# One set of accumulator pools for the whole kernel: keeping three PSUM pairs across the seam into the MLP

## The chip, the cores and the metric

The kernel runs on one core of a Trainium2 chip. The metric is the time of one execution on the device in microseconds (us). The engines are named as in the profile: PE is TensorE (PEld its weight loads), DVE is VectorE, ACT is ScalarE, POOL is GpSimd and SP is SyncE[...]. PE writes its results into a memory of its own, PSUM[...]. In this kernel nearly every PSUM tile is a pair of banks (128 x 2 x 512).

## The reference

Two layers act on `x` of shape (2, 512, 32, 32), all in float32. Cut to what matters:

```python
# layer 0: deformable attention with a bias from a small network, then an MLP
xn = bn(x); q = gconv1x1(xn, qw)
off = tanh(conv1x1(gelu(conv_dw(q)))) * 4
kv = grid_sample(xn, grid(off)); k, v = gconv1x1(kv, kw), gconv1x1(kv, vw)
bias = relu(relu(slog(pos) @ w1 + b1) @ w2 + b2) @ w3 + b3   # 16 groups x 1024 x 64 positions, width 128
attn = softmax(scale * q @ k.T + bias)
x = x + conv1x1(attn @ v, out_w) + out_b
x = x + mlp_w2 @ gelu(mlp_w1 @ bn(x) + mlp_b1) + mlp_b2      # 512 -> 2048 -> 512, 2 x 1024 positions
# layer 1: plain attention over 1024 positions, width 512
q, k, v = x @ Wq.T + bq, x @ Wk.T + bk, x @ Wv.T + bv
x = x + softmax(q @ k.T / sqrt(512)) @ v @ Wp.T + bp
```

## The kernel before

The kernel has four stretches, and a scheduler orders the instructions of each engine; it places all waits on semaphores itself, from what each tile's users are.

*The main loop* (lines 778 to 841) computes the bias network: 256 steps, each of four tiles `ps` (L635) of 128 x 2 x 512 in PSUM, evicted by ACT (L644, L646) and summed by DVE and by adding transfers. The logits are gathered in tiles `sim` of one bank each. Two PSUM pools exist for it, opened at L132: `simp` with two single banks for the logits, and `zp` with three pairs for everything else. In the built program `simp` lies in banks 0 and 1, `zp` in banks 2 to 7.

*The output projection* (`project`, L894) and all later matrix products are done with seven products of half-sized blocks in place of eight (`PARTS`, L98). `multiply` (L116) runs through the products in a given order: it takes a tile from a pool, calls `product`, which issues the matmuls, and then hands the tile to a function that evicts it, mostly a DVE addition (`plus`, L122) or an ACT copy. A product of the projection or the MLP is eight PE instructions. `project(0)` and `project(1)` (L1030, L1037), one for each image of the batch, take their tiles from `zp`, in the order 1, 2, 5, 6, 7, 3, 4.

*The MLP* (loop at L1044) has eight units, four for each image. A unit has `layer1` (L959; order 1, 6, 7, 4, 5, 3, 2, with evictions into `hm` and a gelu on ACT, L962) and `layer2` (L992; order 3, 2, 1, 5, 6, 7, 4). Its tiles come from a third pool, `mq`, of four pairs. It is opened at L1042, after the loop at L1040 has closed `zp` and `simp`, and covers their eight banks. In the built program its first tile is in banks 0 and 1, and the next three are in 6, 4 and 2.

For each unit the loop also prepares a part of layer 1's biases: L1051 transfers 256 KB of a weight into `wr`, and DVE multiplies it by a row and sums it (L1060). `wr` has one buffer, so each transfer waits for the L1060 before it. The scheduler puts all eight of these L1060 early: five of them stand among the evictions of `project(0)` and `project(1)`, and three among those of the first unit's layer 1. The weights of a unit (`w1t`, `w2t`, 1 MB each) are loaded by `load_unit` (L877) and completed by POOL (L105), as is `gg` (L846), 1 MB, which the attention of layer 1 needs later.

*The attention of layer 1* (from L1073) takes its tiles from `mq` as well.

Of the kernel before, what the change touches and what calls it, by code (L numbers as in the profile page):

```python
# [12 lines left out]
PSUM = bass.MemoryType.PSUM  # L13
# [26 lines left out]
for _name, _w in _VCOLS:  # L40
    VOFF[_name] = _n
    _n += _w
NV = _n


@with_exitstack
def conv_seq_kernel(ctx: ExitStack, tc: tile.TileContext, x, xt, kst, pst, cst, vec, wsm, outw, w1, w2, wl, wlt, brow, out):
# [7 lines left out]
    ident = cp.tile([P, P], F32, name="ident")  # L55
    vs = cp.tile([P, NV], F32, name="vs")
    nc.scalar.dma_start(out=vs, in_=vec)
# [71 lines left out]
        x = [q[:, k : k + 2, n : n + 512] for k in (0, 2) for n in (0, 512)]  # L129
        return w + [wsum[:, j] for j in range(3)], x + [parts[:, j] for j in range(3)]  # L130

    simpp, zpp = (tc.tile_pool(name=n, bufs=c, space=PSUM) for n, c in (("simp", 2), ("zp", 3)))  # L132
    simp, zp = simpp.__enter__(), zpp.__enter__()

    def flat(name):
        return zp.tile([P, 2, 512], F32, tag="ps2", name=name).rearrange("p h n -> p (h n)")
# [4 lines left out]
    with tc.tile_pool(name="lp", bufs=2) as lp:  # L141
# [389 lines left out]
        def weights(i):  # L531
            ps = [flat("psg") for _ in range(2)]
            for o in range(NCH):
                for k in range(NCH):
                    if i == 0 and (o, k) in ((1, 0), (3, 1)):
                        yield
                    nc.tensor.matmul(  # L537
                        ps[k // 2][:, k % 2 * 512 : k % 2 * 512 + 512], wls[i][:, 0, o, k * P : (k + 1) * P],
                        wls[i][:, 1, o, :], start=(o == 0), stop=(o == NCH - 1),
                    )  # L540
            yield
            for k2 in range(2):
                nc.scalar.copy(gs[:, i, 2 * k2 : 2 * k2 + 2, :].rearrange("p k o -> p (k o)"), ps[k2])
            yield
            nc.gpsimd.dma_start(out=gdr[i], in_=gs[:, i])
# [4 lines left out]
        head, g, n = chain(0), weights(0), weights(1)  # L550
# [321 lines left out]
    with ExitStack() as top, tc.tile_pool(name="wp", bufs=2) as wp:  # L872
# [4 lines left out]
        def load_unit(b, p):  # L877
            ws_ = []
            for i, w in enumerate((w1, w2)):
                wt = wp.tile([P, 7, 2, 256], F32, name=f"w{i + 1}t")  # L880
                nc.sync.dma_start(out=wt[:, 0:4], in_=w[:, p])
                fold(nc.gpsimd, [wt[:, j] for j in range(7)])
                ws_.append(wt)
            wts[b, p] = ws_

        for i, (b, h) in enumerate(halves):
            for o in range(NCH):
                n = slice(h * 512, (h + 1) * 512)
# [148 lines left out]
        project(1, *op1, op1w[:, 3:5].rearrange("p a k n -> p a (k n)"))  # L1037
        spread([xb[:, j] for j in range(7)])
        load_unit(*units[1])
        for pl in (zpp, simpp):  # L1040
            pl.__exit__(None, None, None)
        mqp = tc.tile_pool(name="mq", bufs=4, space=PSUM)  # L1042
        mq = mqp.__enter__()
        for i, (b, p) in enumerate(units):  # L1044

            j, k = divmod(i, NCH)
# [28 lines left out]
    with tc.tile_pool(name="sp", bufs=1) as sp:  # L1075
# [3 lines left out]
        for b in range(B):  # L1079
# [171 lines left out]
            multiply(mq, (1, 2, 6, 7, 5, 3, 4), product(vt, at, nk=4), {  # L1251
                1: a1, 2: a2, 6: a6, 7: a7, 5: a5, 3: a3, 4: a4,
            })
    mqp.__exit__(None, None, None)


def _constants(np):
# [112 lines left out]
```

## Time and profile before

Three timed runs gave a median of 2648.25 us (2647.37 to 2648.81).

| | |
|---|---|
| time of the profiled execution | 2648.76 us |
| its span on the core | 2647.0 us |
| PE busy | 2628.8 us (99%) |
| DVE busy | 2240.1 us (85%) |
| ACT busy | 1693.2 us (64%) |
| POOL busy | 791.0 us (30%) |
| main loop, about | 0 to 1890 us |
| projection | about 1890 to 1949 us |
| MLP | 1952 to 2339 us |
| attention of layer 1 | 2339 to 2642 us |

A busy share is an average over these four stretches. What one seam costs is read from the engines' timelines around it: when an engine's last instruction ended, when its next one started, and what released it. In the rows of a timeline, a bracket at the end gives the idle time before the row and the instruction or transfer that ended it. Lines of helpers stand for many callers: L123 is every DVE eviction by `plus`, so rows are told apart by the tile they write (`xs` and `op1w` in the projection, `hm` in layer 1 of the MLP).

### The profile page before, as it was taken

What the parts mean: (1) busy time and instruction counts of PE and PEld (TensorE: products, weight loads), DVE (VectorE), ACT (ScalarE), POOL (GpSimd) and SP (SyncE); (2) the same over time, 40 slices, a digit from 0 to 9 for tenths busy, and PEclk for the clock granted to TensorE, in tenths of its full rate; (3) what the DMA queues carried; (4) which work ended last, traced back from release to release, by engine and by line L of the source; (5) the groups of instructions that cost most, each with busy time, mean ns of one, the idle gap of its engine ahead of it and who ended that gap; (6) DMA issues with size and microseconds to landing.
All of it is one profiled execution on the core that took longest, in us unless ns stands there. A gap on an engine that the chain in (4) does not pass through costs nothing.

```text
span 2647.0 us, 46958 instructions
## 1 busy us (share of the span) xinstructions
PE 2628.8 (99%) x19368; PEld 953.9 (36%) x19368; DVE 2240.1 (85%) x1329; ACT 1693.2 (64%) x2222; POOL 791.0 (30%) x867
## 2 busy tenths in 40 slices
PE   9999999999999999999999999999999999999999
PEld 3333322333333233233333323333334444446454
DVE  7999999999999999999999999999674483466354
ACT  5887898888888878887887777777521131114041
POOL 1333333333333333333333333333432232000000
PEclk9999999999999999999999999999999999999999
DMA  5788977888878888887887888788721111000000
GB/s 188 178 178 173 199 166 167 179 182 197 177 169 180 178 178 193 173 177 169 182 183 169 176 177 182 168 174 185 193 96 33 47 48 48 0 17 0 32 1 32
DMA packets 116294, 366.77 MB, mean 139 GB/s; under 512 B 23376, under 2 KB 27616, under 8 KB 113392
## 3 DMA queue, kind: packets, MB, share of 16 engines
q0 software_dynamic: 69408, 235.31, 47.3%
q1 hardware_dynamic: 46240, 128.15, 13.7%
q8 instruction: 153, 2.51, 0.4%
q14 instruction: 61, 0.50, 0.1%
q10 hardware_dynamic: 432, 0.31, 0.0%
HBM read 74.81 MB, written 6.55 MB: 31 GB/s over the span
## 4 chain that ended last, share of the span: by engine, by line
PE 92%; DVE 3%; issue 2%; ACT 2%; DMA 1%; DVEq 0%; POOL 0%; SPq 0%; ACTq 0%; POOLq 0%
PE ps L635 62%; PE sw L953 15%; PE sw L1084 9%; PE sw L1182 2%; PE sim L721 1%; PE psg L537 1%; DVE h L618 1%; PE sw L900 1%; DVE ub L654 0%; DMA wr<-in_wlt 0%; PE pkv L471 0%; DVE xs L908 0%; PE sim L704 0%; PE pt L738 0%; DMA uc<-uo 0%
## 5 line engine op out<-in xcount | busy, mean ns | idle before, releaser
L635 PE MATMUL ps<-h,cw 128*32 128x512 f32 x16384 | 1776.4, 592 | 5.2 <-ACT rx L644 4.0
L618 DVE CUSTOM_DVE_ANT_1 h<-ta,tb 128x4096 f32<-128x4096 f32 (+1 forms) x257 | 1131.2, 4402 | 28.6 <-PE ps L635 25.8
L635 PEld LDWEIGHTS ps<-h,cw 128*32 128x32 f32 x16384 | 543.0, 110 | 1203.1 <-issue 1131.4
L644 ACT ACTIVATE rx<-ps,sc 128x1024 f32<-128x1024 f32 x512 | 567.9, 1109 | 145.1 <-PE ps L635 127.1
L646 ACT ACTIVATE ub<-ps,sc 128x1024 f32<-128x1024 f32 x256 | 308.2, 1204 | 93.6 <-PE ps L635 93.5
L654 DVE SCALAR_TENSOR_TENSOR ub<-rx,sc,ub 128x1024 f32<-128x1024 f32 x256 | 327.1, 1278 | 6.6 <-ACT ub L646 6.6
L673 POOL DMA_DIRECT2D ua<-uc x126 | 158.8, 1275 | 298.6 <-DMA ua<-uc 288.7
L673 POOL DMA_DIRECT2D ua<-ua x189 | 225.9, 1372 | 16.8 <-DMA ua<-uo 11.9
L953 PE MATMUL sw<-xb,w1t 128*128 128x512 f32 x448 | 195.2, 596 | 3.1 <-DVE xs L123 3.1
L656 POOL DMA_DIRECT2D uo<-ub x127 | 125.6, 989 | 233.0 <-DVE ub L654 217.8
L953 PE MATMUL sw<-hm,w2t 128*128 128x512 f32 x448 | 193.6, 592 | 0.0
L646 ACT ACTIVATE uo<-ps,sc 128x1024 f32<-128x1024 f32 x128 | 154.2, 1204 | 53.0 <-PE ps L635 52.7
L654 DVE SCALAR_TENSOR_TENSOR uo<-rx,sc,uo 128x1024 f32<-128x1024 f32 x128 | 163.7, 1279 | 9.0 <-ACT uo L646 9.0
L123 DVE TENSOR_TENSOR hm<-hm,sw 128x1024 f32<-128x1024 f32 x56 | 67.5, 1218 | 105.5 <-PE sw L953 105.3
L673 POOL DMA_DIRECT2D uc<-uo x63 | 53.6, 852 | 313.5 <-DMA uc<-uo 307.4
L953 PEld LDWEIGHTS sw<-xb,w1t 128*128 128x128 f32 x448 | 85.7, 192 | 111.5 <-issue 105.7
L962 ACT ACTIVATE hm<-hm,vs 128x512 f32<-128x512 f32 x64 | 42.5, 713 | 129.0 <-DVE hm L123 129.0
L953 PEld LDWEIGHTS sw<-hm,w2t 128*128 128x128 f32 x448 | 85.1, 190 | 107.1 <-issue 106.4
L123 DVE TENSOR_TENSOR xs<-xs,sw 128x1024 f32<-128x1024 f32 (+1 forms) x48 | 55.6, 1171 | 73.7 <-PE sw L1084 36.0
L656 POOL DMA_DIRECT2D ua<-ub x64 | 58.6, 915 | 179.1 <-DVE ub L654 171.8
L1084 PE MATMUL sw<-aT,vt 128*128 128x512 f32 x224 | 96.7, 593 | 0.3 <-ACT aT L1164 0.3
L987 ACT COPY hm<-sw 128x1024 f32<-128x1024 f32 x8 | 8.1, 1010 | 136.3 <-PE sw L953 136.3
(247 smaller groups left out, 2268.2 us busy)
## 6 DMA issues: line engine op xcount, KB each, us to landing
uo<-ub POOLq DMA_DIRECT2D x127, 512.0 KB, 5.5
fb<-fdr SPq DMA_DIRECT2D x64, 512.0 KB, 5.1
ua<-ub POOLq DMA_DIRECT2D x64, 512.0 KB, 5.5
uc<-ub POOLq DMA_DIRECT2D x64, 512.0 KB, 5.1
ua<-ua POOLq DMA_DIRECT2D x63, 256.0 KB, 6.2
ua<-uo SPq DMA_DIRECT2D x63, 256.0 KB, 2.6
ua<-uo POOLq DMA_DIRECT2D x63, 256.0 KB, 5.7
uc<-uc POOLq DMA_DIRECT2D x63, 256.0 KB, 6.7
```

The lines of the kernel that those rows point to most:

```text
L123: nc.vector.tensor_tensor(out, a, b_, op)
L618: nc.vector._custom_dve(TENSOR_ADD_SAT, out=h1[:, y : y + step].rearrange("p y t x -> p (y t x)"), in0=a.unsqueeze(1).to_broadcast([P, ste ...
L635: nc.tensor.matmul(ps[32 * q : 32 * q + 32, h, :], cw2[:, 32 * z : 32 * z + 32], h1[:, 16 * h : 16 * h + 16, q, :], start=True, stop=True,)
L644: nc.scalar.activation(o, ps, AF.Relu, bias=sc[:, 4 + z : 5 + z])
L646: nc.scalar.activation(o, ps, AF.Relu, bias=sc[:, 4 + z : 5 + z], scale=sc[:, z : z + 1])
L654: nc.vector.scalar_tensor_tensor(r[1], r[0], sc[:, z : z + 1], r[1], ALU.mult, ALU.add)
L656: nc.gpsimd.dma_start(out=sums[s][1], in_=sums[s][3], accum_op=ALU.add)
L673: nc.gpsimd.dma_start(out=out, in_=in_, accum_op=ALU.add)
L953: nc.tensor.matmul(ps[:, m, :], w[:, a, k, m * P : (m + 1) * P], x[:, b_, k, :], start=(k == 0), stop=(k == 1),)
L962: nc.scalar.activation(hm[:, blk, m, :], src[:, m, :], AF.Gelu, bias=col("mb1", 4 * p + 2 * (blk // 2) + m), scale=scale,)
L1084: nc.tensor.matmul(ps[:, m, :], w[:, a, k, c + m * P : c + (m + 1) * P], x[b_][:, k, :], start=(k == 0), stop=(k == nk - 1),)
L1182: nc.tensor.matmul(v[:, m, :], xbl[b_][:, k, m * P : (m + 1) * P], gn[:, a, k, :], start=(k == 0), stop=(k == 1),)
```

## The change

`zp` is opened first and stays open to the end of the kernel; `simp` is opened after it, so that in the built program the pairs lie in banks 0 to 5 and the logits in 6 and 7. At the start of the MLP only `simp` is closed. A pool of one pair is opened in its place, and a small class, `Turns`, takes tiles in turn: one from the new pair, then three from `zp`, and so on. The number of pairs from the MLP on is four, as before.

```diff
+class Turns:
+    def __init__(self, pools):
+        self.pools = pools
+
+    def tile(self, *args, **kw):
+        self.pools = self.pools[1:] + self.pools[:1]
+        return self.pools[-1].tile(*args, **kw)
...
-    simpp, zpp = (tc.tile_pool(name=n, bufs=c, space=PSUM) for n, c in (("simp", 2), ("zp", 3)))
-    simp, zp = simpp.__enter__(), zpp.__enter__()
+    zp = ctx.enter_context(tc.tile_pool(name="zp", bufs=3, space=PSUM))
+    simpp = tc.tile_pool(name="simp", bufs=2, space=PSUM)
+    simp = simpp.__enter__()
...
-        for pl in (zpp, simpp):
-            pl.__exit__(None, None, None)
-        mqp = tc.tile_pool(name="mq", bufs=4, space=PSUM)
-        mq = mqp.__enter__()
+        simpp.__exit__(None, None, None)
+        mq = Turns([ctx.enter_context(tc.tile_pool(name="mq", bufs=1, space=PSUM)), zp, zp, zp])
...
-    mqp.__exit__(None, None, None)
```

## The prediction

> **What bounds the kernel now.** I read the page's busy shares and chain first, then TensorE's waits, then the seam between the projection and the MLP engine by engine. TensorE (PE) is busy 2628.8 of 2647.0 us. From the start of the MLP to the end the chain of waits is almost only matmuls, and it reaches that start by way of a transfer and VectorE (DVE). From the chain in order of time (start, length, what):
>
> ```profile
> 1946.29 4.01 DMA wr<-in_wlt
> ...
> 1951.13 1.14 DVE xs L123
> 1952.27 0.04 issue
> 1952.32 386.35 PE sw L953 x896
> 2338.67 72.10 PE sw L1084 x168
> ```
>
> The waits of PE from 1950 us on (total, times, longest) show the one stall there:
>
> ```profile
> PE sw L953 <- DVE xs L123: 3.1, 1, 3.1
> PE sw L1084 <- ACT aT L1164: 0.3, 2, 0.2
> ```
>
> The timeline of PE (start, duration, count) places it: the last product of `project(1)` (L900), then the first unit's layer 1 (56 instructions are seven products of eight), then its layer 2.
>
> ```profile
> 1945.60 3.60 PE L900 MATMUL sw<-op1x,vp 128*128 128x512 f32 x8
> 1952.32 25.85 PE L953 MATMUL sw<-xb,w1t 128*128 128x512 f32 x56 [3.12 <-DVE xs L123]
> 1978.00 7.46 PE L953 MATMUL sw<-hm,w2t 128*128 128x512 f32 x17
> ```
>
> A second loss hangs on the first. The table of stretches for L953 (length, PE busy, PEld busy, granted clock, DMA share, GB/s) shows the clock halved after the stall:
>
> ```profile
> 1949.20:1952.30 3.10, 0.00 (x0) 0.00 (x0) 0.96 0.81 276
> 1952.30:1955.70 3.40, 3.38 (x5) 1.52 (x6) 0.53 0.97 380
> 1955.70:1959.00 3.30, 3.30 (x9) 1.51 (x8) 1.00 1.04 354
> ```
>
> DVE's timeline through the same time is what decides how much of this can be won:
>
> ```profile
> 1950.43 0.69 DVE L1060 SCALAR_TENSOR_TENSOR wr<-wr,br 128x512 f32<-128x512 f32 x1 [0.77 <-DMA wr<-in_wlt]
> 1951.05 0.08 DVE L1060 DVE_READ_ACCUMULATOR wr<-wr,br 128x1 f32 x1
> 1951.05 1.22 DVE L123 TENSOR_TENSOR xs<-xs,sw 128x1024 f32<-128x1024 f32 x1
> 1961.11 1.22 DVE L123 TENSOR_TENSOR hm<-hm,sw 128x1024 f32<-128x1024 f32 x1 [8.85 <-PE sw L953]
> 1962.38 1.61 DVE L1060 SCALAR_TENSOR_TENSOR wr<-wr,br 128x512 f32<-128x512 f32 x1
> ...
> 1966.74 1.37 DVE L1060 SCALAR_TENSOR_TENSOR wr<-wr,br 128x512 f32<-128x512 f32 x1 [1.05 <-DMA wr<-in_wlt]
> ...
> 1970.87 1.39 DVE L1060 SCALAR_TENSOR_TENSOR wr<-wr,br 128x512 f32<-128x512 f32 x1 [1.61 <-DMA wr<-in_wlt]
> ```
>
> The reader is to see that L1060, a row of work that the MLP doesn't need, stands between the evictions in DVE's queue, and each time waits for a transfer into a single buffer. The transfer for the L1060 of 1962.38 was issued at 1953.12 behind 3 MB of weights (w2t, w1t, gg); the DMA view of 1953 to 1954 us gives its time to landing:
>
> ```profile
> wr<-in_wlt SPq DMA_DIRECT2D x1, 256.0 KB, 9.2
> ```
>
> So it landed at about 1962.3. It was no bound before, since the eviction ahead of it ended at 1962.33.
>
> [...] the idles of 1.67 and 0.81 us at 1927 and 1935 us cost no clock. [...]
>
> **The change part by part.** In the built program every engine has the same instructions in the same order in both kernels; waits differ at six. Before, the first MLP product waits for the last eviction of `project(1)` (DVE, 1951.05 to 1952.27), though its own banks, the logits', had long been free: the new pool waited for all of the old ones. After, product 1 waits for its weights alone. Product 6 (second in order) waits for the eviction of product 7 of the projection (ends 1945.12), product 7 for that of product 3 (1949.66), product 4 for the last (1952.27). ScalarE (ACT) drops its DVE wait before copying product 1. One L1060 gains a wait for the L1060 before it, done at 1951.13; I cost it at nothing, the hm eviction ahead of it ends later, and at most a 0.05 us queue row if not.
>
> *Gain at the seam.* Products follow each other every 3.43 us (1938.73 to 1942.16), so PE could go on at 1945.60 + 3.43 = 1949.03, and starts at 1952.32: 3.29. In the slow clock, from the first matmul to that of the second product takes 5.09 us (second product at 1952.32 + 5.09 = 1957.41 by its weight loads, 0.43 apart), against 3.51 after the short stall at 1935.22 (next product 1938.73): 1.58. Filling the pipeline again is the other 0.08. Sum 4.95. No new buffer wait follows: PE wants the buffers of products 6, 7 and 4 at 1952.46, 1955.89 and 1959.32, all later than their evictions. The inputs are older still: normalised xb is complete at 1940.7, the folded w1t at 1915.8.
>
> *What is late next.* Layer 1 would end, and layer 2 want to begin, at 1949.03 + 7 x 3.43 = 1973.04. Its first matmul reads hm[3], so it needs ACT's gelu (L962), which needs the first DVE eviction of product 5, which stands behind three L1060 in DVE's queue. The first hm eviction moves from 1961.1 to 1956.0, but the L1060 behind it still can't start before 1962.3 (landing) and takes 1.61. It frees the buffer, and the next transfer lands 2.6 us later (1966.7); L1060 takes 1.37; again a transfer (1970.9) and 1.39. This chain is tied to the transfers and not to PE, so it doesn't move: the eviction of product 5 starts at 1972.18 and the gelu at 1973.43 as before. From ACT:
>
> ```profile
> 1973.43 1.33 ACT L962 ACTIVATE hm<-hm,vs 128x512 f32<-128x512 f32 x2 [2.80 <-DVE hm L123]
> ```
>
> Two halves of 0.71 us lie in that row; PE needs the first at its start: 1973.43 + 0.71 + 0.05 of handover (as from 1952.27 to 1952.32 in the chain) = 1974.2. The second ends at 1974.76, PE reaches it at 1975.1. So PE stalls 1974.2 - 1973.04 = 1.2 us, and with the 0.08 of refilling gives back 1.25. After that the evictions of products 3 and 2 are done at about 1975.7 and 1976.9 and the gelu of hm[0] at 1978.4, before PE wants it at 1981.1; the other units have no L1060, and their loads are issued when PE frees a buffer, so they move with it.
>
> *Sum.* 4.95 - 1.25 = 3.70 us. The profiled execution took 2648.76 us (span 2647.0 and 1.76 around it): 2645.06. The three timed runs have a median of 2648.25, 0.51 lower; less 3.70 that is 2644.55. I take 2644.8, between them.
>
> **The rivals.** *A, the whole 4.95 is won:* the wr transfer lands 1.2 us or more earlier. For it: the DMA rate already falls to some 50 GB/s at 1960 us, so little is left to move then. Against: nothing in the change moves the transfer or its issue. 2648.76 - 4.95 = 2643.8, by the median 2643.3. *B, the stall only moves:* the transfer lands 2 us later, the new stall is above 3 us, and the clock drops there too: 4.95 - 3.2 - 0.08 - 1.58 = 0.1 gained, 2648.7. For it: it was issued into full queues and its delay is no fixed number. Against: the queues were empty from 1962.0 on (0 GB/s in a table of stretches), and the two later transfers take 2.6 each. *C, slower:* the pairs move from banks 2-7 to 0-5 and the logits from 0-1 to 6-7, in the whole main loop. Were an eviction or a matmul group dearer there, it counts 1024 times (512 + 256 + 128 of the page's ACT rows, and more in rows it leaves out). The gain is gone at 3.70 / 1024 = 3.6 ns a tile; at 10 ns the time is 2648.76 - 3.70 + 10.24 = 2655.3. Against: L635 on three pairs and L953 on all four, the logits' place included, both have 592 ns a matmul. Unknown from both sides, below nothing too; I take zero.
>
> **How the numbers follow.** Main case 0.63, A 0.18, B 0.13, C 0.06. About 0.2% (5.3 us) is what a measurement of this kernel can tell from no change; faster by more than that means below 2642.95, which none of the cases gives by its own sum, so it takes A and a low run, or the main case with gains I don't see: 0.12. C gives slower: 0.06. The rest, 0.82, is within. The range, 2643.0 to 2647.2, holds the main case with a landing 1.2 us earlier to 2 us later without the clock drop (2643.8 to 2647.1) and A by the median.
>
> **What would show it.** Right: the first L953-type matmul starts at about 1949.0, the clock stays at 1.00 there, the first L1060 after the first hm eviction now waits for its transfer (about 5 us), and a new PE stall of about 1.2 us before layer 2, released by ACT's gelu. Wrong: a PE start above 1950, a clock below 1 after the seam, layer 2 beginning at 1973.1 (A) or after 1975.5 (B), or another time at 1945 us (C).

## The result, and the profile after

| | before | after |
|---|---|---|
| median of 12 runs each, us | 2649.26 | 2645.77 |
| lowest to highest, us | 2646.70 to 2651.06 | 2643.40 to 2648.08 |
| time of the profiled execution, us | 2648.76 | 2645.56 |
| its span, us | 2647.0 | 2643.8 |

The ratio of the times is 0.9984, with a 95% interval of 0.9977 to 0.9992: 0.16% faster, which is within the 0.2% band, as forecast. One later execution of the changed kernel, of 21 in e10, ran at a clock of 0.556 and took 4672.46 us; the ratios are taken without it. Lines of the changed kernel are 12 higher than before (11 for the evictions: L123 became L134). The lines that answer to those shown of before follow.

The chain of waits of the changed kernel (start, length, what) now runs from the projection into the MLP with nothing between matmuls; the transfer and the DVE pieces that stood before the MLP are gone.

```profile
1939.58 11.16 PE sw L912 x26
1950.73 384.71 PE sw L965 x896
2335.44 72.10 PE sw L1096 x168
```

TensorE's waits after 1940 us (total, times, longest): the 3.1 us on the eviction is no longer there.

```profile
PE sw L1096 <- ACT aT L1176: 0.3, 2, 0.2
```

Its timeline (start, duration, operation, count) gives the two distances that matter. The MLP starts 1950.57 - 1947.14 = 3.43 us after the last product, which is one product. Layer 2 starts 1974.70 - 1950.57 = 24.13 us later, where seven products take 24.03.

```profile
1947.14 3.60 PE L912 MATMUL sw<-op1x,vp 128*128 128x512 f32 x8
1950.57 24.20 PE L965 MATMUL sw<-xb,w1t 128*128 128x512 f32 x56
1974.70 10.54 PE L965 MATMUL sw<-hm,w2t 128*128 128x512 f32 x24
```

The table of stretches for L965 (length, PE busy, weight loads, granted clock, DMA share, GB/s) has the full clock, where before had 0.53:

```profile
1950.50:1953.90 3.40, 3.33 (x8) 1.52 (x8) 1.00 0.82 274
1953.90:1957.30 3.40, 3.40 (x9) 1.52 (x8) 1.00 1.00 389
```

DVE's timeline (the bracket is the idle time before a row, and what ended it) shows the sums, now L1072, late behind their transfers, as the prediction said:

```profile
1957.71 1.22 DVE L134 TENSOR_TENSOR hm<-hm,sw 128x1024 f32<-128x1024 f32 x1 [4.17 <-PE sw L965]
1962.68 1.72 DVE L1072 SCALAR_TENSOR_TENSOR wr<-wr,br 128x512 f32<-128x512 f32 x1 [3.75 <-DMA wr<-in_wlt]
...
1967.19 1.34 DVE L1072 SCALAR_TENSOR_TENSOR wr<-wr,br 128x512 f32<-128x512 f32 x1 [1.65 <-DMA wr<-in_wlt]
...
1971.27 1.39 DVE L1072 SCALAR_TENSOR_TENSOR wr<-wr,br 128x512 f32<-128x512 f32 x1 [1.60 <-DMA wr<-in_wlt]
```

And ACT's gelu of hm[3], which layer 2 needs first:

```profile
1973.84 1.33 ACT L974 ACTIVATE hm<-hm,vs 128x512 f32<-128x512 f32 x2 [2.80 <-DVE hm L134]
```

Half of this row is done after 0.71 us, and 0.05 us of handover makes 1974.60. TensorE could begin layer 2 at 1950.57 + 24.03 = 1974.60. The two meet: the 1.25 us that the prediction takes off for this wait isn't lost here, though the chain behind it is there in full.

What lies ahead of the seam was 1.54 us later in this execution (last projection product at 1947.14 against 1945.60): the projection began 1.17 us later (1896.54 against 1895.37) and took 0.37 longer. In the main loop, which the change doesn't touch but for the place of its banks, TensorE was busy 395.45 us of the stretch 200 to 600 us against 397.03. So 3.2 us of span are gained, though the seam itself gained 4.8. Repetitions of either kernel spread over 4 us, so single spans can't settle a term of 1 us; the distances around the seam can.

### The profile page after: what moved, and what is told of

The parts are those of the page before. It is cut to its first block, busy times and chain, and to the rows that moved or that the text cites. A ratio compares the mean times of both kernels' runs of the same rounds, so it can differ in the third digit from the quotient of the medians.

```text
span 2643.8 us, 46960 instructions
## 1 busy us (share of the span) xinstructions
PE 2626.8 (99%) x19368; PEld 942.7 (36%) x19368; DVE 2240.6 (85%) x1329; ACT 1692.8 (64%) x2222; POOL 791.8 (30%) x867
## 4 chain that ended last, share of the span: by engine, by line
PE 93%; DVE 3%; ACT 2%; issue 2%; DMA 0%; DVEq 0%; ACTq 0%
PE ps L647 62%; PE sw L965 15%; PE sw L1096 9%; PE sw L1194 2%; PE sim L733 1%; PE psg L549 1%; PE sw L912 1%; DVE h L630 1%; DVE ub L666 0%; DVE xs L920 0%; PE pkv L483 0%; PE sim L716 0%; PE pt L750 0%; DVE acc L346 0%; ACT ub L658 0%
## 5 line engine op out<-in xcount | busy, mean ns | idle before, releaser
L647 PEld LDWEIGHTS ps<-h,cw 128*32 128x32 f32 x16384 | 532.4, 110 | 1215.5 <-issue 1140.4
L965 PE MATMUL sw<-hm,w2t 128*128 128x512 f32 x448 | 193.6, 592 | 0.0
L965 PE MATMUL sw<-xb,w1t 128*128 128x512 f32 x448 | 193.6, 592 | 0.0
L134 DVE TENSOR_TENSOR hm<-hm,sw 128x1024 f32<-128x1024 f32 x56 | 67.4, 1218 | 98.0 <-PE sw L965 97.6
L965 PEld LDWEIGHTS sw<-hm,w2t 128*128 128x128 f32 x448 | 85.0, 190 | 107.4 <-issue 106.4
L965 PEld LDWEIGHTS sw<-xb,w1t 128*128 128x128 f32 x448 | 85.1, 190 | 107.1 <-issue 105.2
L134 DVE TENSOR_TENSOR xs<-xs,sw 128x1024 f32<-128x1024 f32 (+1 forms) x48 | 55.6, 1170 | 72.9 <-PE sw L1096 36.0
L610 ACT ACTIVATE ta<-fb,vs 128x512 f32<-128x512 f32 (+1 forms) x65 | 89.3, 1376 | 10.8 <-DMA fb<-fdr 10.8
```

The source lines that it names most:

```text
L134: nc.vector.tensor_tensor(out, a, b_, op)
L610: nc.scalar.activation(ta.rearrange("p j x -> p x j")[:, :, j0:j1], fb[:, 0, :, j0:j1], AF.Identity, bias=col("cb1"), scale=col("w1x"),)
L647: nc.tensor.matmul(ps[32 * q : 32 * q + 32, h, :], cw2[:, 32 * z : 32 * z + 32], h1[:, 16 * h : 16 * h + 16, q, :], start=True, stop=True,)
L965: nc.tensor.matmul(ps[:, m, :], w[:, a, k, m * P : (m + 1) * P], x[:, b_, k, :], start=(k == 0), stop=(k == 1),)
```

## The experiments

They are read by two distances. The first goes from the start of the projection's last product to the start of layer 2. Without any loss it is 3.43 + 24.03 = 27.46 us; what is above that is lost at the seam or before layer 2 ("lost"). The second ("whole") goes from the start of the projection's first product to the start of layer 2, and so has the stalls of the projection in it too. The last column says where the slow clock shows: after the longest stall of the projection (at about 1928 us), where eight matmuls then took 5.40 us and not 3.70, or at the start of the MLP, where the table of stretches has 0.53. Starts in us, from TensorE's timeline of each profile:

| kernel | first product | last product | MLP | layer 2 | lost | whole | slow clock |
|---|---|---|---|---|---|---|---|
| before | 1895.37 | 1945.60 | 1952.32 | 1978.00 | 4.94 | 82.63 | MLP |
| before, a second execution (e7) | 1895.97 | 1947.03 | 1952.64 | 1978.47 | 3.98 | 82.50 | both |
| before, banks as after (e1) | 1895.72 | 1946.93 | 1952.95 | 1977.09 | 2.70 | 81.37 | projection |
| before, stall filled (e2) | 1895.61 | 1946.95 | 1953.61 | 1977.75 | 3.34 | 82.14 | none |
| before, late sums (e8) | 1896.75 | 1948.25 | 1953.16 | 1977.30 | 1.59 | 80.55 | projection |
| after | 1896.54 | 1947.14 | 1950.57 | 1974.70 | 0.10 | 78.16 | none |
| after, a second execution (e0) | 1895.62 | 1946.82 | 1950.25 | 1974.28 | 0.00 | 78.66 | none |
| after, a third (e10) | 1898.12 | 1949.58 | 1953.01 | 1977.04 | 0.00 | 78.92 | projection |
| after, more stores (e4) | 1895.07 | 1945.29 | 1948.73 | 1973.33 | 0.58 | 78.26 | none |
| after, late sums (e3) | 1895.50 | 1946.96 | 1950.39 | 1974.42 | 0.00 | 78.92 | projection |
| four pairs in the projection (e5) | 1895.13 | 1942.70 | 1946.14 | 1973.00 | 2.84 | 77.87 | none |
| four pairs, late sums (e6) | 1896.08 | 1943.32 | 1946.76 | 1970.79 | 0.01 | 74.71 | none |
| the same, a second execution (e9) | 1897.84 | 1945.07 | 1948.51 | 1972.54 | 0.01 | 74.70 | none |

The two distances are needed together, because a loss can move from the projection to the seam. TensorE's last product comes later where the projection had its slow clock, while the last eviction that DVE owes it comes no later (it ended 56.6 to 57.2 us after the projection's first product in before, e7 and e1 alike); the stall at the seam is then shorter, and nothing is won by that. In the mean of three executions of each kernel (before, e7 and e1 against after, e0 and e10) the whole fell from 82.17 to 78.58 us, by 3.59, which is what the medians show.

My theory was that of the prediction: the stall and the clock are won, and the sums in DVE's queue give 1.25 us back before layer 2. The rivals were A (nothing is given back), B (the stall moves to layer 2 and costs the clock there) and C (the new bank places cost something in each tile).

### The changed kernel again, twice (e0, e10)

> The changed kernel once more, for how far its seam varies. Theory (the gain is the seam's stall of 3.3 us and the slow clock's 1.6 us; what is given back depends on when the sixth wr transfer lands): the first MLP matmul starts 3.43 us after the last projection product, clock 1.00, and layer 2 starts 24.0 to 25.3 us after that, 24.0 where the transfer lands less than about 12.1 us after the first MLP matmul, 25.3 where it lands 13.3 us after it. Rival (the gain sits elsewhere, in the main loop or the banks): the seam varies by microseconds, or the main loop ends earlier than before's 1890 us.

> The changed kernel again beside these two, for its ratio on the same chip: 0.9977 to 0.9992 as measured first; in its profile layer 2 24.0 to 24.5 us after layer 1 starts (a stall before layer 2 of at most 0.4 us, where the prediction said 1.2).

One execution gave 2645.05 us. The third profile came with 20 more timed runs: 2645.47 us median of all 21, ratio 0.9985 (0.9978 to 0.9992), as at first. Neither lost anything before layer 2. So in the three executions of the changed kernel that were profiled, the give-back is 0.0 to 0.1 us, not 1.25.

### Only the bank places (e1)

```diff
-    simpp, zpp = (tc.tile_pool(name=n, bufs=c, space=PSUM) for n, c in (("simp", 2), ("zp", 3)))
+    zpp, simpp = (tc.tile_pool(name=n, bufs=c, space=PSUM) for n, c in (("zp", 3), ("simp", 2)))
...
-        for pl in (zpp, simpp):
+        for pl in (simpp, zpp):
```

> Before with the banks of the changed kernel alone (pairs in banks 0 to 5, logits in 6 and 7), all pools still closed and a new one opened at the seam. Theory (bank places cost nothing, the gain is the seam): the time of before, ratio 1.000 within 0.0007; PE stalls 3.1 us at the seam and the clock is near 0.5 for 3.4 us. Rival (the gain or a loss is in the banks): 0.998 as the changed kernel, or above 1.001.

2649.43 us, ratio 0.9998 (0.9990 to 1.0006). The upper end is 0.0006 x 2649 = 1.6 us, over 1024 tiles at most 1.6 ns a tile; rival C needed 3.6 to take the gain away. It is out. The experiment says nothing of the cause of the stall: every wait in the built program is as before, and the MLP's first tile is again in banks 0 and 1, which are now those of the projection's last product, so here its own banks call for the same wait.

The profile brought something else. A stall of 3.1 us with a slow clock was expected. The stall is still there, but shorter, and no slow clock follows it. TensorE's timeline, then the table of stretches for L953:

```profile
1946.93 3.60 PE L900 MATMUL sw<-op1x,vp 128*128 128x512 f32 x8
1952.95 24.30 PE L953 MATMUL sw<-xb,w1t 128*128 128x512 f32 x56 [2.42 <-DVE xs L123]
```

```profile
1952.90:1956.30 3.40, 3.35 (x8) 1.63 (x9) 1.00 0.96 400
```

### The kernel before again (e7)

> The kernel before once more, to see how constant its losses at the seam are. The profile read for the prediction had a stall of 3.1 us and then 3.4 us at a clock of 0.53; the kernel with its pairs in other banks had 2.4 us and no slow clock. If the length of the stall decides: a stall near 3.1 us comes with a slow clock, one under 2.5 us without. [...] Span 2645 to 2648 us.

2649.23 us. The stall was shorter still, 2.01 us, and the clock did drop:

```profile
1947.03 3.60 PE L900 MATMUL sw<-op1x,vp 128*128 128x512 f32 x8
1952.64 26.00 PE L953 MATMUL sw<-xb,w1t 128*128 128x512 f32 x56 [2.01 <-DVE xs L123]
```

```profile
1952.60:1956.00 3.40, 3.36 (x4) 1.41 (x5) 0.53 0.99 390
```

The same execution had a slow clock already in the projection, after a shorter stall still, and the changed kernel had none there after a longer one. Eight matmuls took 5.40 us in the first and 3.70 in the second:

```profile
1928.06 5.40 PE L900 MATMUL sw<-qa,vp 128*128 128x512 f32 x8 [1.86 <-DVE xs L123]
1928.83 3.70 PE L912 MATMUL sw<-qa,vp 128*128 128x512 f32 x8 [2.06 <-DVE xs L134]
```

So the length of the stall alone doesn't decide: 1.86 us was enough here and 2.42 was not in e1. What else does isn't shown by these runs. The loss at this seam before was 4.94, 3.98 and 2.70 us in three executions with the same order of instructions (before, e7 and e1), 3.87 in the mean. The prediction's 4.95 is the worst of the three.

The timed runs give no place for a drop, only the mean clock of the whole kernel. One drop (3.4 us at 0.53) lowers it by 3.4 x 0.47 / 2647 = 0.0006; among the 13 profiles, those with no drop have a mean clock of 1.000 (e0 alone 0.999), those with one 0.999 and the one with two 0.998. Of the 102 runs of before that stood beside the experiments, 28 have 1.000, 51 have 0.999 and 23 have 0.998, with mean times of 2648.4, 2649.6 and 2651.0 us. Of the 53 timed runs of the changed kernel with and without late sums (after, e10 but for the one of 4672.46 us, e3), which have the projection's stalls and not that of the seam, 34 have 1.000, 19 have 0.999 and none has 0.998.

### Filling the stall (e2)

```diff
+        fill = flat("wake")
+        with tc.issue_after(newest(PE)):
+            for n in (512, 512, 512, 256):
+                nc.tensor.matmul(fill[:, 0:n], qa[:, 0, 0, 0:P], qa[:, 0, 0, 0:n], start=True, stop=True)
         for pl in (zpp, simpp):
```

The product is not used. It stands between `project(1)` and the MLP.

> Before with four unused matmuls (3.0 us) into a free pair between the last projection product and the MLP; they fill the stall and leave its end where it is. Theory (the slow clock follows from the idle PE and costs 1.6 us beside the stall): the MLP starts about 6.7 us after the start of the last projection product as before, but at clock 1.00, its second product 3.4 us after its first instead of 5.1, and layer 2 comes 1.6 us earlier; ratio 0.9994. Rival (the first products of the MLP are slow for another reason, new weights or pools): the first 3.4 us still run at about half clock, ratio 1.000.

2648.45 us, ratio 0.9996 (0.9988 to 1.0005): unclear. In its profile the filler took 3.17 us in the stall and layer 1 ran at the full clock (24.14 us to layer 2), as expected; but e1 had the full clock there without a filler, so one profile can't show that the filler did it. None of its 12 timed runs has a clock of 0.998, against 6 of the 25 of before beside it. That fits a gain of about 1 us from the clock, but the interval doesn't show it.

### Late sums in the kernel before (e8)

```diff
+            with tc.issue_after(newest(mybir.EngineType.DVE)):
-            nc.vector.scalar_tensor_tensor(
+                nc.vector.scalar_tensor_tensor(
```

Each sum now stands behind the newest DVE work of its unit. The pools are those of before.

> The kernel before, with its pools as they are, and only the L1060 sums put late: none of them is left among the evictions of the projection or of the first unit's layer 1. Theory: the stall of 2.0 to 3.1 us at the seam is in part the last eviction itself (1.22 us) and for the rest DVE's backlog, in which the fifth L1060 waits for its transfer; without the sums the last eviction starts as soon as its product has ended, as it does in the changed kernel with late sums (1950.56 to 1950.59 us), so TensorE's stall falls to 1.2 to 1.4 us, with no slow clock after it. Ratio to before 0.9990 to 0.9995. Layer 2 follows 24.1 us after layer 1 starts. Rival (the stall is the closing of the pools and nothing of it the backlog): a stall of 2 to 3 us as before, ratio 1.0000.

2647.13 us, ratio 0.9991 (0.9983 to 1.0000). TensorE's stall at the seam fell to 1.31 us:

```profile
1948.25 3.60 PE L900 MATMUL sw<-op1x,vp 128*128 128x512 f32 x8
1953.16 24.30 PE L953 MATMUL sw<-xb,w1t 128*128 128x512 f32 x56 [1.31 <-DVE xs L123]
```

DVE's timeline tells why. The last eviction of the projection, the second row, now waits for TensorE, and not TensorE for a backlog:

```profile
1948.93 1.22 DVE L123 TENSOR_TENSOR xs<-xs,sw 128x1024 f32<-128x1024 f32 x1
1951.89 1.22 DVE L123 TENSOR_TENSOR xs<-xs,sw 128x1024 f32<-128x1024 f32 x1 [1.74 <-PE sw L900]
```

So with no backlog the closing of the pools costs one eviction and its handover, 1.3 us. The other 0.7 to 1.8 us of the stall of before went with the sums in DVE's queue, the same ones that the prediction saw only behind the seam. Not all of that is time won: e8's projection had its slow clock, so its last product came late. Counted from the projection's first product the MLP started after 56.41 us, against 56.67 to 57.23 in before, e7 and e1, which is 0.3 to 0.8 us. Some 2 us of the medians (2649.15 to 2647.13) come without touching a pool, though the interval just reaches 1. The rest of them would be the slow clock that no longer follows the shorter stall: none of e8's 13 timed runs has 0.998, against 6 of the 34 of before beside it. That part is inferred.

### More traffic ahead of the sixth transfer (e4)

```diff
+    scr = dp.tile([P, 4, 512], F32, name="scr")
...
+        with tc.issue_after(newest(mybir.EngineType.SP)):
+            for o in range(4):
+                nc.sync.dma_start(out=scr[:, o, :], in_=xs[:, 2 + o % 2, 1, 512:1024])
```

1 MB of stores that nothing reads, in the changed kernel.

> The changed kernel with 1 MB of additional stores (four of 256 KB into an unused DRAM tile) ahead of gg and of the sixth wr transfer. Theory (the L1060 in VectorE's queue tie layer 2 to the wr transfers, with no more than a few tenths of slack): the sixth transfer lands about 2.8 us later (1 MB at 370 GB/s), and PE stalls 2 to 4 us before layer 2 of the first unit, released by ScalarE's gelu[...]. Rival (the chain has slack and the give-back of 1.25 us was only computed): no stall there, layer 2 starts 24.0 us after the MLP.

One execution: 2643.93 us. The transfer landed later: the sum behind it started at 1965.49 after waiting 5.04 us, 15.2 us after the start of the fifth sum, where the changed kernel has 11.0. That is 4.2 us more; the 2.8 expected were an estimate at 370 GB/s, which lies between the 354 and 380 of the prediction's table of stretches. And a stall came before layer 2, released by ACT's gelu, but of 0.41 us:

```profile
1973.33 12.26 PE L966 MATMUL sw<-hm,w2t 128*128 128x512 f32 x28 [0.41 <-ACT hm L975]
```

The expected 2 to 4 us were missed because the scheduler changed DVE's order with the edit: two evictions of hm stood ahead of the first late sum, not one, so that product 5's was behind two sums and not three. The mechanism is seen; its price isn't tested cleanly here.

### Late sums in the changed kernel (e3)

The edit of e8, in the changed kernel.

> The changed kernel with every L1060 sum put behind DVE's newest instruction of its unit, so that none stands among the evictions of the projection or among the first unit's layer 1 evictions. My theory (the give-back hangs on the L1060s in DVE's queue, and in the changed kernel it was just missed): no hm eviction of the first unit waits behind a transfer; the gelu of hm[3] is done 3 us or more before TensorE wants it; layer 2 starts 24.0 to 24.1 us after layer 1 as in the changed kernel, so this gains 0 to 0.1 us at the MLP. In the projection DVE is rid of five sums of 0.7 us and of two waits of 1.6 and 0.5 us: TensorE's stalls there (2.1 and 0.8 us) shrink by 0 to 1 us, since they end at 1928 to 1936 us, mostly before those sums. Ratio to the kernel before 0.998, within 0.0005 of the changed kernel's. Rival (the sums still cost the changed kernel its 1.25 us and the profile only misses it): 1.2 us more gained, layer 2 at 24.0 us after layer 1 either way, ratio 0.9975 or less.

2645.28 us, ratio 0.9983 (0.9977 to 0.9990), as the changed kernel. The sums cost the changed kernel nothing that can be measured, though the gelu of hm[3], with its first half done at 1969.02 + 0.71 = 1969.7, is now 4.7 us ahead of layer 2. The rival with 1.2 us more gained is out.

### Four pairs already in the projection (e5), and with late sums (e6, e9)

```diff
+        simpp.__exit__(None, None, None)
+        one = ctx.enter_context(tc.tile_pool(name="mq", bufs=1, space=PSUM))
+        mq = Turns([zp, one, zp, zp])
...
-                multiply(zp, (p,), go, took)
+                multiply(mq, (p,), go, took)
...
-        simpp.__exit__(None, None, None)
-        mq = Turns([ctx.enter_context(tc.tile_pool(name="mq", bufs=1, space=PSUM)), zp, zp, zp])
```

The first hunk stands where the main loop's logits end, before the projection.

> The changed kernel with the logits' pool closed before the projection and the fourth pair opened there, so that the projection too takes four pairs in turn. Theory: TensorE's stalls in the projection (2.1 and 0.8 us in the changed kernel, each on a DVE eviction of the product three before) fall below 0.5 us in all, since the wait is then for the product four before, 3.4 us earlier. The MLP then starts 2.5 us earlier against VectorE, and the L1060 chain, tied to its transfers, is late for layer 2: a stall of 0.5 to 2.5 us before layer 2, released by ACT's gelu, which is the give-back that I predicted for the change itself. Net 0.5 to 2.5 us under the changed kernel: ratio to before 0.9970 to 0.9982. Rival (the transfers move with the seam, as rival A had it): no stall before layer 2, the whole 2.5 us won, ratio 0.9973. Other rival (DVE is the bound in the projection, so the stall only moves to a later product): ratio 0.9984 as the changed kernel.

> Both edits together: four pairs from the projection on, and the L1060 sums late. Theory: no stall in the projection above 0.5 us and none before layer 2 (24.0 to 24.1 us after layer 1 starts); 2.5 to 3 us under the changed kernel, ratio to before 0.997 to 0.9975, and under the kernel with four pairs alone by what that loses before layer 2 (0.5 to 2.5 us). Rival (no give-back through the L1060 sums): equal to the kernel with four pairs alone.

> Four pairs from the projection on and late sums, once more beside the changed kernel on one chip, since its first timing had only 7 runs (2641.96 us). If that was no accident: 3 to 4 us under the changed kernel, ratio to before 0.9970 to 0.9976, no stall of TensorE between 1895 us and layer 2. Otherwise within 1 us of the changed kernel.

| | median, us | ratio to before | before beside it, us |
|---|---|---|---|
| e5 | 2646.42 | 0.9990 (0.9983 to 0.9996) | 2649.68 |
| e6 | 2641.96 | 0.9972 (0.9961 to 0.9983) | 2649.68 |
| e9 | 2642.24 | 0.9970 (0.9959 to 0.9981) | 2649.15 |

In e5 the stalls of TensorE in the projection (2.1 and 0.8 us) are gone. From the start of the projection's first product to that of its last it takes 47.57 us (from 1895.13), against 50.60 in the changed kernel (from 1896.54; 51.20 and 51.46 in its other two profiles). Most of that is given back before layer 2. TensorE's timeline:

```profile
1942.70 3.60 PE L915 MATMUL sw<-op1x,vp 128*128 128x512 f32 x8
1946.14 24.20 PE L968 MATMUL sw<-xb,w1t 128*128 128x512 f32 x56
1973.00 12.26 PE L968 MATMUL sw<-hm,w2t 128*128 128x512 f32 x28 [2.67 <-ACT hm L977]
```

DVE's timeline of e5 has the chain of the prediction, a sum waiting for its transfer between every two evictions, and the first one for 7.36 us:

```profile
1953.28 1.22 DVE L134 TENSOR_TENSOR hm<-hm,sw 128x1024 f32<-128x1024 f32 x1 [0.91 <-PE sw L968]
1961.85 0.85 DVE L1072 SCALAR_TENSOR_TENSOR wr<-wr,br 128x512 f32<-128x512 f32 x1 [7.36 <-DMA wr<-in_wlt]
...
1965.52 1.31 DVE L1072 SCALAR_TENSOR_TENSOR wr<-wr,br 128x512 f32<-128x512 f32 x1 [1.68 <-DMA wr<-in_wlt]
...
1969.58 1.38 DVE L1072 SCALAR_TENSOR_TENSOR wr<-wr,br 128x512 f32<-128x512 f32 x1 [1.61 <-DMA wr<-in_wlt]
```

ACT's gelu starts at 1972.13. The prediction's formula puts layer 2 at 1972.13 + 0.71 + 0.05 = 1972.89 us, 2.72 later than 1946.14 + 24.03; the trace has it at 1973.00. The clock stayed at 1.00 in this profile, but only 7 of e5's 21 timed runs have a mean clock of 1.000, against 14 of 21 in e3 beside it. Its runs at 1.000 take 2645.3 us in the mean and those at 0.999 2647.8. Its projection has no stall left, so that would be the clock dropping after the stall before layer 2, as in rival B; no profile caught it there. This, and a stall a little above the 0.5 to 2.5 us expected, is why the expected ratio of 0.9970 to 0.9982 was missed.

In e6 the sums are out of the way, and the same TensorE timeline has neither stall:

```profile
1943.32 3.60 PE L915 MATMUL sw<-op1x,vp 128*128 128x512 f32 x8
1946.76 24.20 PE L968 MATMUL sw<-xb,w1t 128*128 128x512 f32 x56
1970.79 14.76 PE L968 MATMUL sw<-hm,w2t 128*128 128x512 f32 x34
```

All 14 timed runs of e6 and e9 have a clock of 1.000. Together they are the best version here, 6.9 to 7.7 us under before and 3.2 under the changed kernel on the same chip (e9 against e10). Their whole distance of 74.7 us is free of loss but for 0.01 at the seam and is 7.5 under the mean of before. Neither of the two edits gave that alone: four pairs alone ended no better than the changed kernel (0.9990 against 0.9984 and 0.9985, with intervals that overlap), and late sums alone beside it.

## Why the prediction was right, point by point

*The time.* 2644.8 us was predicted with a range of 2643.0 to 2647.2; it is 2645.77. The fall is 3.49 us on the first medians and 3.68 on the later ones (2649.15 to 2645.47), against 3.70 predicted. That the sum is so close is in part luck: two of its terms are too large, one on the side of the gain and one on the side of the loss, and they cancel.

*The signs named beforehand.* The clock of 1.00 at the seam came, and so did the sum's wait for its transfer after the first hm eviction (3.75 us, not 5). The MLP started above 1950 us, which was named as a sign of being wrong, but only because everything ahead of it was 1.54 us later; the 3.43 us behind the last product are those predicted. The stall of 1.2 us before layer 2 did not come.

*Stall at the seam, 3.29 us.* Shown. The MLP starts 3.43 or 3.44 us after the last product in every profile of a kernel with the new pools. The reason given, that the new pool waited for all of the old ones, is right: the two built programs differ in six waits and in banks alone, the banks cost nothing that can be measured (e1, ratio 0.9998), and in the changed kernel nothing of the stall is left, though the sums stand in DVE's queue as before. What the prediction left out is what sets its length: with the pools as before, 1.3 us of it stay when DVE has no backlog of sums (e8). The stall itself varies, 3.1, 2.4 and 2.0 us in three executions. It ends with DVE's chain, at 1952.3 to 1952.9 us in all of them, while TensorE's last product started up to 1.4 us apart. It was latest in the two that had the slow clock in the projection.

*Slow clock, 1.58 us.* A term that was mis-sized upward. From the start of the MLP to layer 2 it took 25.68 and 25.83 us where the drop came and 24.14 where it didn't, so a drop costs 1.5 to 1.7 us; but of three executions with this stall one had none. The prediction booked the full price from the one profile that it had. The 0.08 us that it puts down to a pipeline filling again is 3.51 - 3.43, a product after the stall at 1935 us against one without; the difference is measured, its cause is not shown. An estimate from the mean clocks of e7's section: before has (51 + 2 x 23) / 102 = 0.95 drops in a run and the kernels without the seam's stall 19 / 53 = 0.36, so 0.6 drops or 0.9 us are gained. With the shorter stalls, the gain at the seam is 3.87 us in the mean of three, not 4.95, and 3.59 over the whole distance.

*Given back, 1.25 us.* The step that failed, as the prediction put it: "This chain is tied to the transfers and not to PE, so it doesn't move". It isn't tied to TensorE, as e5 shows, but nor is it fixed in time. It begins with the fifth sum, and from its start to the start of the gelu of hm[3] took 1973.43 - 1950.43 = 23.0 us in before and 1973.84 - 1951.71 = 22.1 in after. The sixth sum could start 11.9 us after the fifth did in before and 10.97 in after: the transfer between them is issued behind 3 MB of w2t, w1t and gg, and its time to landing was no fixed number (9.2 us in before, 8.6 in after and 8.3 in e0, against 2.6 for the quickest of the later ones). And the fifth sum came 1.14 us after the MLP's start in after, against the 1.40 that the prediction had (1950.43 - 1949.03). Together 1.1 to 1.2 us, which is the whole of the stall. That is the condition of rival A: the landing 12.1 us after the MLP's start, not 13.3. In the first profile of the changed kernel the gelu was ready just when TensorE wanted it; in e0 and e10 it was ready 0.9 and 1.5 us early. In e0 the sixth sum took 0.76 us in place of 1.72; in e10 the projection's slow clock had held TensorE back, so that the fifth sum came only 0.29 us after the MLP's start. By how much the unprofiled runs missed the stall can't be said.

*Rival A* therefore has the mechanism for the step before layer 2, but not its time, since it too books the full clock. *Rival B* didn't come in the changed kernel; in e5 the stall of 2.67 us came where B puts it, and the mean clocks (14 of 21 runs at 0.999) fit its slow clock. *Rival C* is out by e1.

*Costs put at nothing.* The waits of products 6, 7 and 4 for their buffers: TensorE waits for nothing between 1947 us and layer 2. The added wait of one sum for another: no such wait is seen in DVE's rows, each sum waits for its transfer or not at all.

*What stays open.* Why the clock drops after one stall of about 2 us and not after the next. The stall at the seam and the slow clock behind the projection's stall aren't independent (in the three profiles with the old pools and the sums early, the one is shorter where the other came), and three profiles of each kernel can't fix a mean to better than some tenths of a us; so how the gain of 3.5 to 3.7 us divides between stall and clock is an estimate. The slow clock in the projection is still there in the changed kernel: e10's profile has it, and 10 of e10's 21 runs are at 0.999.

## What to carry to other kernels

When a stall is to be taken away, look for the next deadline behind it and for the chain that has to meet it. If that chain is tied to transfers, its slack has to be counted from the event that starts it, and over more than one execution: here 1.2 us of slack appeared that one profile didn't show, and in e5 most of the 3 us that were won in the projection were lost again to the same chain. A stall that looks shorter in one execution isn't a gain until the stretch ahead of it has been counted too. Work that nobody waits for (here the sums) belongs behind the evictions in an engine's queue, all the more when it waits for a single-buffered transfer; moving it and giving the projection the fourth pair, on top of the change, gave twice the gain of the change alone.

## What the runs showed that was not expected

- After 1.86 and 2.01 us of idle TensorE in e7 and after 2.00 in e1 the clock fell: at e7's seam to a mean of 0.53 over the next 3.4 us, and in the projections of e7 and e1 eight matmuls took 5.40 us and not 3.70. After 2.06 us in after, 2.42 in e1 and 2.67 in e5 it stayed at 1.00 over the next 3.4 us. After 2.5 us in e0 nothing but the stall itself was lost: from the projection's first product to its last e0 takes 0.6 us more than after (51.20 against 50.60), and its two stalls there are longer by as much.
- The same sum of 128x512 values takes DVE 0.68 to 0.69 us in the projection, while POOL runs no fold, and mostly longer while POOL runs its folds of w2t, w1t and gg. In before the folds run from 1955.81 to 1971.70 us, and the three sums that start in that time take 1.61, 1.37 and 1.39 us; in after from 1956.23 to 1972.11, and they take 1.72, 1.34 and 1.39. In e7 the folds end at 1970.51: the two sums ahead of that take 1.19 and 1.25 us and the third, at 1970.96, takes 0.69. In e10 the sixth sum took 0.95 us during a fold of w1t, so a fold doesn't set the length alone; why it grows isn't shown. In the first unit this lengthens the chain before layer 2: its three sums take 4.45 us together in after.
- Executions of one kernel with one order of instructions put the start of the MLP up to 2.8 us apart (1950.25 to 1953.01 in three of the changed kernel), which is nearly the whole gain of the change.
